# Two pre-activation layers on one core: the softmax without its maximum, checked after the fact instead of bounded beforehand

## The chip, the core and the metric

The kernel runs on one core of a Trainium2 chip. A core has a matrix engine (PE, with its weight loads shown as PEld), a vector engine (DVE), a scalar engine (ACT), GpSimd (POOL) and SyncE (SP), which in this kernel only issues transfers. Time is device time in microseconds (us). Each engine works through its own list of instructions in order; between engines, semaphores make one wait for another.

## The reference

The input x is 4 images of 16 channels of 256 x 256, in f32. Two layers, each of the form x + layer(GroupNorm(x)) with 8 groups of two channels:

```python
def _L0_conv_ref(x, conv_w, conv_b):          # conv_w: (16*25, 16, 3, 3)
    out = conv(x, conv_w, padding='SAME') + conv_b[None, :, None, None]
    logits = out.reshape(N, C, K * K, H, W)   # K = 5
    weights = jax.nn.softmax(logits, axis=2)
    return jnp.einsum('ncuij,ncuij->ncij', _unfold(x), weights)

x = x + _L0_conv_ref(_gn(x), L0_conv_conv_w, L0_conv_conv_b)
x = x + _L1_conv_ref(_gn(x), ...)   # silu and cubic B-splines of 3x3 patches, weighted sums, bias
```

`_unfold(x)` holds the 5 x 5 neighbourhood of each pixel. In layer 0 every pixel of every channel has 25 logits of its own, so the softmax is over 25 x 16 x 4 x 65,536 numbers. The second layer takes x1, the first layer's result.

## The kernel before, in words

**Prologue.** All four images are read for their group statistics. Image 0 comes in two halves of 2 MB that are kept (`held`), images 1 to 3 go through three buffers (`xin`); `load_x` (L498) issues them, five at the start and each further one when a half has been used. For each half DVE takes `bn_stats` (L635, L637); per image `group_stats` turns them into mean and rstd over two small matmuls with `ones` and a power on POOL (L165), from which the factors `nrm` and `nrz` follow (L655 to L658). At the same time the program finds a bound of the logits. ACT squares each half (`xq`, L644), 16 matmuls with an identity add the squares over the channels (`sq`, L647), DVE takes the maximum (`hm`, L650). The weights' squares (`aw`, `wps`) are summed once. From both, a chain of small operations (L660 to L690) computes whether every logit is small enough for an exponential without a maximum: `flag`.

Between these, `normalize` for the upper half of image 0 advances a piece at a time (`ahead`, two calls of `next` per group). It writes normalised x to DRAM in two layouts: by rows (`hs`, put from SP at L329) for the neighbourhoods, and transposed by columns (`hst`, and `hsl` with a high and a low part, L343) for the convolution. It uses two xp buffers and two buffers each of the transposed tiles.

**The branch.** Every engine loads `flag` (L1387) and branches (L1391). One arm runs both layers without a maximum, `layer0(False)`, the other runs both with it, `layer0(True)`, `layer1("g", ...)`. Only one arm runs.

**Layer 0.** 64 strips (4 images x 2 halves of 128 rows x 8 strips of 32 columns), rows on partitions, each strip in 8 steps of 4 columns. In each step PE makes the logits of 4 columns, two pairs with 2 matmuls a column (L974, L978), in three PSUM buffers; ACT takes the exponentials of each pair (L997); POOL multiplies them by the neighbourhood `u` (L1002); one step later (LAG) DVE adds numerators and denominators over the 25 (L813). `e`, which holds exponentials and products, has four buffers. After a strip follow, a few steps later each, `seed` (ACT: Ln and Exp of the denominators, L827, L829, an approximate reciprocal), `divide`, `refine`, `quotient` (DVE, L833 to L844), and per block of 128 columns `apply` (adds y to x in a transfer that POOL issues, L851), `store` (x1 to DRAM, L913) and `statistics` (ACT: sums of x1 and of its squares with accumulated output, L876). `step()` runs such delayed work when it is due, then `next(ahead)` advances `normalize` of the next image: densely, with a piece in every step, while image 0's strips run, more spread out for images 2 and 3. `x1` is stored from SP, but for the last strip.

SP issues, in the order of the program: columns `am` (four transfers) and `an` (one) for each half strip of 16 columns (L750, L758), `u` for each strip (L771), `xc` blocks (L791), xp loads (L321), and the puts of `normalize`. Two `an` buffers have rows of ones, set by DVE at the start of the layer (L736). `in_order` fixes the order of each engine's instructions within the two layers as written.

**Layer 1.** 64 units of 16 rows. Splines of x1 are built on DVE, ACT and POOL, and PE adds 3 x 3 convolutions (L1304, L1313). `scales(b, ...)` computes x1's group statistics for images 2 and 3 along the way, as pieces of the chain `more`. Outputs are stored by SP.

## Time and profile before

| what | us |
|---|---|
| three runs | 2863.25, 2865.0, 2867.84 (median 2865.0) |
| the profiled execution | 2861.58, of which span 2859.8; granted PE clock 0.982 |
| VectorE busy | 2774.1 (97%) |
| TensorE busy | 2716.4 (95%) |
| GpSimd busy | 2666.5 (93%) |
| ScalarE busy | 2124.1 (74%) |
| first transfer of columns `am` issued | 105.98 |
| first reduce of layer 0 starts | 125.61 |
| seed of the last strip | 1988.82 |
| last work on VectorE ends | 2853.5 |
| last store issued | 2854.77 |

The span runs from the first to the last instruction of the profiled execution; the device time beside it is that of the same execution. In a line of groups the columns are: line, engine, operation, output and inputs with their shapes, count, then busy time and the mean length of one (ns), then the idle time of the engine just before them and what ended most of it. A chain of waits is followed back from the last instruction, to what released each. A row of stretches gives busy times and, in brackets, numbers of instructions of each engine. Layer 0 starts at about 106 us and ends at about 1990, layer 1 follows it with some overlap on ACT and POOL.

### The profile page before, as it was taken

How to read it: one execution, taken by the hardware profiler on the slowest of the kernel's cores; microseconds unless marked ns; L12 is line 12 of the kernel's file. 1: busy time of each engine (PE TensorE's matmuls, PEld its weight loads, DVE VectorE, ACT ScalarE, POOL GpSimd, SP SyncE). 2: the span in 40 equal slices, each digit the busy share in tenths (PEclk: the TensorE clock that was granted, in tenths of full speed). 3: DMA queues.
4: the chain of work that ended last, by engine and by line, in shares of the span. 5: the costliest groups of instructions: out<-in, count | busy, mean ns of one | idle time of the engine just before them, and what ended most of it. 6: DMA issues, size and time to landing. Idle time of an engine off the chain costs nothing.

```text
span 2859.8 us, 39212 instructions
## 1 busy us (share of the span) xinstructions
PE 2716.4 (95%) x14282; PEld 1483.3 (52%) x14282; DVE 2774.1 (97%) x1821; ACT 2124.1 (74%) x2737; POOL 2666.5 (93%) x1096
## 2 busy tenths in 40 slices
PE   4699999999999999999999999996999999999999
PEld 3466666666666666666666666663343333323222
DVE  7699999999999999999999999999999999999996
ACT  6566777667767567676664655647999999999995
POOL 4399999999999999999999999999899999999995
PEclk8799999999999999999999999998999999999999
DMA  9877999979989779898886674866778787787783
GB/s 289 260 232 228 286 293 287 274 231 263 277 242 299 232 231 259 243 296 244 256 249 181 195 226 146 244 196 195 233 244 254 244 259 246 247 258 247 255 246 106
DMA packets 337663, 692.96 MB, mean 242 GB/s; under 512 B 29554, under 2 KB 254276, under 8 KB 287092
## 3 DMA queue, kind: packets, MB, share of 16 engines
q1 hardware_dynamic: 329796, 658.13, 74.5%
q0 software_dynamic: 7664, 32.23, 5.5%
q8 instruction: 115, 1.88, 0.3%
q14 instruction: 88, 0.72, 0.1%
HBM read 533.16 MB, written 121.15 MB: 229 GB/s over the span
## 4 chain that ended last, share of the span: by engine, by line
DVE 52%; PE 22%; issue 10%; ACT 6%; DMA 5%; POOL 2%; SPq 1%; DVEq 0%; POOLq 0%; ACTq 0%
DVE nd L813 42%; PE yp L1304 12%; PE lg L974 6%; PE yp L1313 3%; DVE ring L181 3%; DVE s L178 2%; PE lg L978 2%; DVE r L837 1%; DVE y L844 1%; DVE nd L833 1%; POOL e L1002 1%; DVE r1a L1148 1%; ACT xta L1139 1%; DMA xp<-in_x_dram 1%; ACT xtc L1139 1%
## 5 line engine op out<-in xcount | busy, mean ns | idle before, releaser
L1002 POOL TENSOR_TENSOR e<-e,u 128x1600 f32<-128x1600 f32 x512 | 1806.0, 3818 | 45.0 <-ACT e L997 27.8
L813 DVE TENSOR_REDUCE nd<-e 128x128 f32<-128x3200 f32 x512 | 1757.9, 3489 | 20.5 <-POOL e L1002 20.5
L974 PE MATMUL lg<-wm,am 128*128 128x400 f32 x4096 | 1731.6, 503 | 45.3 <-ACT e L997 33.3
L978 PE MATMUL lg<-wn,an 96*128 96x400 f32 x2048 | 1341.6, 655 | 0.8 <-DMA an<-hsl 0.8
L997 ACT ACTIVATE e<-lg 128x800 f32<-128x800 f32 x1024 | 810.3, 835 | 627.2 <-DVE nd L813 504.3
L974 PEld LDWEIGHTS lg<-wm,am 128*128 128x128 f32 x4096 | 750.7, 191 | 386.3 <-ACT e L997 113.1
L1304 PE MATMUL yp<-ring,wt 128*32 128x512 f32 x6144 | 721.2, 595 | 33.9 <-DVE ring L181 33.3
L978 PEld LDWEIGHTS lg<-wn,an 96*128 96x128 f32 x2048 | 386.0, 188 | 307.2 <-DMA an<-hsl 3.3
L1304 PEld LDWEIGHTS yp<-ring,wt 128*32 128x32 f32 x6144 | 227.9, 109 | 493.1 <-issue 429.3
L1161 POOL TENSOR_TENSOR s1b<-s1b,r1a 128x1024 f32<-128x1024 f32 (+1 forms) x96 | 192.6, 2038 | 0.0
L1161 POOL TENSOR_TENSOR s1a<-s1a,r1a 128x1024 f32<-128x1024 f32 (+1 forms) x96 | 192.3, 2037 | 0.0
L181 DVE SCALAR_TENSOR_TENSOR ring<-s,s1a 128x1024 f32<-128x1024 f32 x132 | 156.6, 1210 | 0.9
L181 DVE SCALAR_TENSOR_TENSOR ring<-s,s1b 128x1024 f32<-128x1024 f32 (+1 forms) x128 | 153.5, 1225 | 0.3
L876 ACT ACTIVATE z<-xc,nrm 128x256 f32<-128x256 f32 x240 | 144.3, 601 | 4.0
L1161 POOL TENSOR_TENSOR s1a<-s1a,r1b 128x512 f32<-128x512 f32 (+2 forms) x68 | 119.7, 1792 | 0.0
L1161 POOL TENSOR_TENSOR s1b<-s1b,r1b 128x512 f32<-128x512 f32 x64 | 114.8, 1820 | 0.0
L178 DVE SCALAR_TENSOR_TENSOR s<-xta,cb,s 128x1024 f32<-128x1024 f32 (+2 forms) x90 | 112.2, 1272 | 0.5 <-issue 0.4
L1157 POOL TENSOR_TENSOR s1a<-r1b 128x1536 f32<-128x1536 f32 (+1 forms) x31 | 86.7, 2795 | 26.2 <-ACT r1b L1146 26.2
L178 DVE SCALAR_TENSOR_TENSOR s<-xtb,cb,s 128x1024 f32<-128x1024 f32 (+2 forms) x85 | 107.2, 1287 | 1.9 <-ACT s L175 1.9
L178 DVE SCALAR_TENSOR_TENSOR s<-xtc,cb,s 128x1024 f32<-128x1024 f32 (+2 forms) x85 | 107.0, 1285 | 0.0
L175 ACT ACTIVATE s<-xta,cb 128x1024 f32<-128x1024 f32 (+2 forms) x90 | 96.4, 1085 | 12.5 <-DVE ring L181 11.0
L1157 POOL TENSOR_TENSOR s1b<-r1b 128x1536 f32<-128x1536 f32 (+1 forms) x32 | 86.4, 2699 | 17.5 <-ACT r1b L1146 17.5
(211 smaller groups left out, 2258.8 us busy)
## 6 DMA issues: line engine op xcount, KB each, us to landing
am<-hst SPq DMA_DIRECT2D x508, 259.8 KB
u<-hs SPq DMA_DIRECT2D x64, 1440.0 KB
an<-hsl SPq DMA_DIRECT2D x127, 519.5 KB
xta<-x1s SPq DMA_DIRECT2D x40, 1024.0 KB
xtb<-x1s SPq DMA_DIRECT2D x40, 1024.0 KB
xtc<-x1s SPq DMA_DIRECT2D x40, 1024.0 KB
x1s<-xc SPq DMA_DIRECT2D x30, 1024.0 KB
hs<-hsp SPq DMA_DIRECT2D x32, 576.0 KB
```

What stands on the lines that cost most here:

```text
L175: nc.scalar.activation(s, t, AF.Square, scale=-0.5, bias=cb)
L178: nc.vector.scalar_tensor_tensor(p, t, cb2, s, ALU.subtract, ALU.mult)
L181: nc.vector.scalar_tensor_tensor(f, p, 0.0, q, ALU.min, op)
L813: nc.vector.tensor_reduce(nd[:, :, :, j : j + JG].rearrange("p t c j -> p t j c"), e.rearrange("p t j m c d -> p t j c m d"), AX.XY, ALU.add,)
L876: nc.scalar.activation(z, v, f, scale=nrm[b][:, 0, g : g + 1], bias=nrm[b][:, 1, g : g + 1], accum_out=st1[b][:, t, g, columns_of(n) : col ...
L974: nc.tensor.matmul(lg[:, i, :NL], lhsT=am[:, o : o + P], rhs=wm.rearrange("p m c d -> p (m c d)"), start=True, stop=False,)
L978: nc.tensor.matmul(lg[:, i, :NL], lhsT=an[:, o : o + P], rhs=wn.rearrange("p m c d -> p (m c d)"), start=False, stop=True,)
L997: nc.scalar.activation(ev, lg[:, :, :NL], AF.Exp)
L1002: nc.gpsimd.tensor_tensor(e[:, 1].rearrange("p j m c d -> p j (m c) d"), e[:, 0].rearrange("p j m c d -> p j (m c) d"), uv, ALU.mult,)
L1157: nc.gpsimd.tensor_tensor(s1(n, a, z), r1(n, a, z), r1(n, a, z), ALU.mult)
L1161: nc.gpsimd.tensor_tensor(s1(n, a, z), s1(n, a, z), r1(n, a, z), ALU.mult)
L1304: nc.tensor.matmul(yp[t * M : (t + 1) * M], lhsT=wt[:, d, e].rearrange("p r o -> p (r o)"), rhs=ring[:, r0 + t * RT + d : r0 + t * RT + d ...
```

## The change

The bound and the branch ahead of the layers are taken out. Both layers run at once without a maximum; the sums are recorded and checked, and at the very end a branch repeats both layers with the maximum if the check fails.

- The prologue loads and measures images 0 and 1 alone, four loads of 2 MB. `xq`, `sq`, `hm`, `aw`, `wps`, `ms`, `bd` and all their work are gone.
- Images 2 and 3 are measured in layer 0, by a new generator `measure`, while images 1 and 2 have their strips: xp loads from SP, per group and half three ACT instructions (Identity with accumulated sum, a Copy of one element, Square with accumulated sum), then two small matmuls, DVE operations and a power on POOL. It pauses while `statistics` are due. `normalize` of the same image follows it in the chain, now dense for all images.
- `seed` gets a Copy over the denominators that accumulates their sum, a small bias in Ln, and an accumulated sum in Exp. The sums go to `seen`.
- `verdict`, in layer 1's chain `more` after `scales`, compares `seen` with 1e30 and computes `flag` (DVE, one matmul, DVE).
- `ubrow` moves from a lasting pool to the prologue's, `zero` becomes smaller with a broadcast source.

The stores of x1 are issued as before.

```diff
+    def factors(b, mean, rstd):
+        nc.vector.tensor_copy(nrm[b][:, 0], rstd)
+        nc.vector.scalar_tensor_tensor(nrm[b][:, 1], mean, -1.0, rstd, ALU.mult, ALU.mult)
+        nc.gpsimd.tensor_mul(nrz[b][:, 0], rstd, gsel_sb)
+        nc.vector.scalar_tensor_tensor(nrz[b][:, 1], rstd, EPS, rstd, ALU.mult, ALU.mult)
+
+    def measure(b, ptr, tiles, busy):
...
+        for h in range(NH):
+            load(0, h)
+        for _ in range(3):
+            yield
+        for q in range(C // QC):
+            for h in range(NH):
+                for k in range(QC // GC):
+                    while busy():
+                        yield
...
+                    nc.scalar.activation(v, v, AF.Identity, accum_out=s)
+                    nc.scalar.activation(m, s, AF.Copy, scale=-1.0 / n)
+                    nc.scalar.activation(v, v, AF.Square, bias=m, accum_out=s)
+                    yield
+                load(q + 1, h)
...
+        nc.tensor.matmul(
+            ps[0], lhsT=ones, rhs=moments[:, 0].rearrange("p g h -> p (g h)"),
+            start=True, stop=True,
+        )
+        yield
+        nc.vector.tensor_reduce(
+            mean, ps[0].rearrange("p (g h) -> p g h", h=NH), AX.X, ALU.add
+        )
+        nc.vector.tensor_scalar(mean, mean, -1.0 / NH, None, ALU.mult)
+        nc.vector.tensor_tensor(
+            d, moments[:, 0], mean.unsqueeze(2).to_broadcast([P, G, NH]), ALU.add
+        )
+        nc.vector.tensor_mul(d, d, d)
+        nc.vector.scalar_tensor_tensor(d, moments[:, 1], 1.0 / n, d, ALU.mult, ALU.add)
+        yield
+        nc.tensor.matmul(
+            ps[1], lhsT=ones, rhs=d.rearrange("p g h -> p (g h)"), start=True, stop=True
+        )
+        yield
+        nc.vector.tensor_reduce(
+            var, ps[1].rearrange("p (g h) -> p g h", h=NH), AX.X, ALU.add
+        )
+        nc.vector.tensor_scalar(var, var, 1.0 / NH, EPS, ALU.mult, ALU.add)
+        yield
+        nc.gpsimd.tensor_tensor(rstd, var, mhalf, ALU.pow)
+        yield
+        factors(b, mean, rstd)
+        yield
+
+    def verdict(psum):
+        low = seen.rearrange("p t n -> p (t n)")
+        least = stat1.tile([P, 1], F32, name="least")
+        nc.vector.tensor_scalar(low, low, 1e30, None, ALU.is_lt)
+        nc.vector.tensor_reduce(least, low, AX.X, ALU.min)
+        yield
+        ps = psum()[:, 0:1]
+        nc.tensor.matmul(ps, lhsT=ones, rhs=least, start=True, stop=True)
+        yield
+        bad = stat1.tile([1, 1], F32, name="bad")
+        nc.vector.tensor_scalar(bad, ps[0:1], 1.0 - 0.5 / P, None, ALU.is_lt)
+        nc.vector.tensor_copy(flag, bad)
+        yield
...
-        loaded = [load_x(n) for n in range(5)]
+        loaded = [load_x(n) for n in range(2 * NH)]
...
-        for b in range(B):
+        for b in range(2):
...
-                nc.scalar.activation(xq, t, AF.Square)
-                sq = pstat.tile([P, W], F32, name=f"sq_{n}", tag="sq")
-                for c in range(C):
-                    nc.tensor.matmul(
-                        sq, lhsT=idr, rhs=xq[:, c], start=c == 0, stop=c == C - 1
-                    )
-                nc.vector.tensor_reduce(hm[:, n : n + 1], sq, AX.X, ALU.max)
                 next(ahead, None)
-                if n >= NH and n + 3 < B * NH:
-                    loaded.append(load_x(n + 3))
...
             def seed(n, nd, xc):
                 r = prc.tile([P, C, SW], F32, name=f"r_{n}{arm}", tag="r")
-                nc.scalar.activation(r, nd[:, 0], AF.Ln)
+                nc.scalar.activation(
+                    nd[:, 0], nd[:, 0], AF.Copy, accum_out=seen[:, 1, n : n + 1]
+                )
+                nc.scalar.activation(r, nd[:, 0], AF.Ln, bias=tiny)
                 seeds[:1] = [newest(ACTE)]
-                nc.scalar.activation(r, r, AF.Exp, scale=-1.0)
+                nc.scalar.activation(
+                    r, r, AF.Exp, scale=-1.0, accum_out=seen[:, 0, n : n + 1]
+                )
...
-                    ahead = normalize(b + 1, ptr, tiles, dense=b == 0) if b + 1 < B else iter(())
+                    ahead = iter(())
+                    if b + 1 < B:
+                        ahead = normalize(b + 1, ptr, tiles, dense=True)
+                        if b > 0:
+                            ahead = chain(measure(b + 1, ptr, tiles, summing), ahead)
...
-    fast = nc.values_load(
+    layer1("", *layer0(False))
+    bad = nc.values_load(
         flag[0:1, 0:1], min_val=0, max_val=1,
         skip_runtime_bounds_check_because="a comparison's result",
     )
-    with tc.If(fast > 0) as small_logits:
-        layer1("", *layer0(False))
-    with small_logits.Else():
+    with tc.If(bad > 0):
         layer1("g", *layer0(True))
```

## The prediction, made before the changed kernel had run

> **What bounds the kernel now.** I read the engine table, the chain of waits, the groups, the busy time by stretches, then the waits of VectorE (DVE) and the timeline at the places that the change touches.
>
> ```profile
> DVE 52%; PE 22%; issue 10%; ACT 6%; DMA 5%; POOL 2%; SPq 1%; DVEq 0%; POOLq 0%; ACTq 0%
> ...
> L1002 POOL TENSOR_TENSOR e<-e,u 128x1600 f32<-128x1600 f32 x512 | 1806.0, 3818 | 45.0 <-ACT e L997 27.8
> L813 DVE TENSOR_REDUCE nd<-e 128x128 f32<-128x3200 f32 x512 | 1757.9, 3489 | 20.5 <-POOL e L1002 20.5
> ...
> L997 ACT ACTIVATE e<-lg 128x800 f32<-128x800 f32 x1024 | 810.3, 835 | 627.2 <-DVE nd L813 504.3
> ```
>
> ```profile
> 0.00:50.00 50.00, 17.95 (x78) 15.76 (x78) 32.94 (x131) 26.93 (x33) 31.80 (x85) 0.93 0.96 281
> 50.00:100.00 50.00, 29.00 (x138) 25.27 (x138) 38.17 (x125) 41.78 (x64) 3.79 (x5) 0.66 0.93 294
> ...
> 286.00:572.00 286.00, 276.53 (x990) 180.74 (x988) 280.90 (x109) 212.77 (x378) 276.88 (x88) 0.99 0.98 285
> 572.00:858.00 286.00, 282.52 (x1003) 181.33 (x1002) 286.00 (x110) 200.79 (x334) 285.02 (x88) 1.00 0.85 253
> ```
>
> Columns of the second view: stretch, length, busy time (instructions) of PE, PE loads, DVE, ACT, POOL, granted clock, DMA share, GB/s. In layer 0 DVE decides: from 572 on it is busy 286.00 of 286. ACT waits 504 us for DVE, so added ACT work is free as long as no single delay uses up the pipeline's lead. Layer 0 has 512 steps; 28.94 us a strip of eight gives 3.617 a step. At 916.1 a reduce frees an e buffer; exps end 1.6 us later, the POOL product takes 3.5, the reduce 3.4 and hand-overs about 0.5: 9.0 of the 14.5 us that four buffers last, so the **lead is about 5.5 us**. Before 125.61 there is no reduce: the prologue is a serial 126 us, to which this chain belongs:
>
> ```profile
> 99.93 1.65 POOL rstd_x L165
> ...
> 104.72 0.15 DVE flag L690
> 104.89 0.50 POOLq L1387
> ...
> 106.64 0.58 SPq L750
> ...
> 117.47 10.68 DMA xp<-in_x_dram
> ```
>
> Image 3's statistics end at 101.6, bound and flag take until 104.87, the branch about 1.1, and only then are layer 0's columns (am) loaded; the first matmul is at 111.04, the first product at 122.06 (after u, issued at 112.46).
>
> **The change, part by part.**
>
> *Prologue.* Gone are five squares of 3.62 on ACT in 36 to 100 (18.1 us) with aw (1.06), DVE's statistics of images 2 and 3 (four halves of 8 x 0.61, about 19), the squares' matmuls, four of six 2 MB loads (8.4 MB at 290 GB/s, 29 us of DMA in a stretch with a share of 0.93), and the tail 99.93 to 105.98. What stays sets the new end: ACT is busy 55.66 us in 36 to 100, without squares and aw 36.5. Image 0's factors, at 35.76 now, come about 2 us sooner. So ACT ends no sooner than 34 + 36.5 = 70.5; its waits for DVE there (2.77, 1.43, 1.02, 2.20, 0.69) add 8.1: 78.6. The last put and its landing take some 6 more (98.33 to 105.98 now holds 1.4 us of ACT and put, the rest is covered): am at about 86 instead of 105.98, **-20**. Bounds: if DVE's waits go too, -28; if the pace of tile buffers and puts (two buffers, each put waited for) holds and only tail and one square in two go, -11. The two an memsets (1.79 each) move to where DVE is free; moved ubrow memsets and ident are not on the path.
>
> *Layer 0, DVE.* Measuring images 2 and 3 puts ten small DVE operations per image between reduces. Their like in the prologue (L155 to L163, L655 to L658) take 0.15 to 0.19 and start 0.2 apart: 1.75 an image, **+3.5** (2.4 to 4), all on the path.
>
> *Layer 0, ACT.* A measured step holds two exps (1.57 together at 287.32) and Identity and Square over 512 elements (0.58 each as L827), two accumulator reads, bounded by this row's 0.19,
>
> ```profile
> L876 ACT ACTIVATION_READ_ACCUMULATOR z<-xc,nrm 128x1 f32 x240 | 46.4, 193 | 0.0
> ```
>
> and a one-element Copy (0.20 as L382): 1.75, with gaps up to 2.15. 3.3 to 3.7 against 3.617: ACT has no spare time over 16 steps an image, and every eighth step a seed takes 2.2 instead of 1.2 (a Copy over 512 and two reads more). Each xp buffer is reloaded after its second step and read again two steps later. Cycle: 14.47 us of four steps, less one step (3.62) and 1.8 of work, leaves 9.0 for the load; the two loads that the chain of waits holds took 10.68 (at 117.47, share 0.81) and 17.97 (at 277.49, share 0.98). I take 10.68, since the stretch had 0.85: three reloads late by 1.7 are 5.0, within the lead of 5.5. **+1** for both images (0 to 43: three times 9.0 less 5.5, twice). The seed's extra 1.0 in the other strips is hidden by ACT's waiting.
>
> *Layer 0, SyncE.* The reload of an image's lower half waits in SP for ACT's fourth measured step, and the next block's four am and one an are queued behind it. PE frees their buffer just before that step's exps, so they go out up to 1.57 + 2.15 = 3.7 later than now. They last until the next block, 14.5 us on; from first issue to first matmul they took 5.1 (105.98 to 111.04). The sum, 8.8, is covered: 0; were loads as slow as 10.7, 14.4 would still just be covered. The stores of x1 stand in the same queue as before: 0.
>
> *Layer 0, PE and POOL.* The second ones-matmul stands two steps after the first, behind DVE's deviations: PE gives up its lead and sits idle some 7 us. What follows is seen at 288.89, where ACT waited 6.65 us for xp:
>
> ```profile
> 297.18 1.70 PE L974 MATMUL lg<-wm,am 128*128 128x400 f32 x2 [4.40 <-ACT e L997]
> ```
>
> This and the next pair took 1.70 and 1.47 instead of 0.84. After the deviations DVE holds two reduces (7.0); the next product needs two slow pairs of columns (3.3), an exp (0.85), the product (3.5) and 0.3: 7.95. About 1 late. POOL's power (1.65) then eats POOL's regained lead, 0.3 more. **+2.6** for two images (0 to 6).
>
> *Layer 0, dense normalisation of images 2 and 3.* Image 1 is dense now: DVE waits 5.1 us for POOL in 286 to 572, at a DMA share of 0.98. Images 2 and 3, spread out, show none. Part of the 5.1 is that one late xp load. **+4** for two (0 to 10.2).
>
> *Layer 1 and end.* The last strip's divide already waits 1.28 for ACT (1990.04); the seed's extra Copy lies in it: **+1.0** (0 to 1.3). The verdict's four DVE operations and its matmul stand in units where DVE and PE are both full: **+0.7** (0 to 1.2). The flag's load and branch now stand behind all: now from the flag's end (104.87) to the first instructions behind (105.51 to 106.24) it took 0.65 to 1.4; partly under the last store's flight (2854.77 to 2859.8): **+0.5** (0 to 1.4).
>
> The Trainium skill, "Advanced Engine Details and Errata", "Control Flow Timing", gives a compare-and-branch as about 108 ns. The rows above are six to thirteen times that, since load and synchronisation are in them; by the page the last term would be 0.1 and the sum 0.4 lower.
>
> **Sum**: -20 + 3.5 + 1 + 2.6 + 4 + 1.0 + 0.7 + 0.5 = -6.7. The profiled execution took 2861.6 (span 2859.8, the rest around it) and would take 2854.9; it lies 3.4 under the median of 2865.0, against which runs are compared: 2858.3, rounded **2858**.
>
> **Rivals.**
> *The prologue gives only half* (-10): puts and SyncE's queue, not ACT, set its end. For it: two tile buffers, ACT waiting for DVE in five places; weight loads ws wait in SP among large loads (up to 4.06 us each). Against: those waits fall with the loads. -10 + 13.3 = +3.3: 2868.
> *ScalarE uses up the lead* while it measures. Place: the 16 steps of images 2 and 3, at the xp reload; it decides once a reload takes over 9.0 + 5.5/3 = 10.9 us. For it: 10.68 is just below, 17.97 well above. Against: mean share 0.85. At 14.3, midway, 3 x 5.3 - 5.5 = 10.4 an image: +21 instead of +1, so **2878, slower**.
> *The change doesn't do what it says*: the sums fail their test and both layers are run again. Then the time is over 5,500. For these inputs, normalised logits of a few units, exponentials are far from 1e30; nothing in the trace shows them.
>
> **How the numbers follow.** About 0.2% (5.7 us) is what a measurement here can tell from no change: faster is below 2859.3, slower above 2870.7. Forecast 0.50 (of it 0.40 faster, 0.10 within), half a prologue 0.25 (0.03, 0.15, 0.07), ScalarE 0.24 (0, 0.03, 0.21), repetition 0.01. Faster 0.43, within 0.28, slower 0.29. The forecast's own range is 2846 to 2868 (prologue -28 with the sum's other terms low but not all at zero, and -14 with them near the values taken plus 3). The whole range reaches to the second rival: 2846 to 2879.
>
> **What would show it.** First am issue near 86 and first reduce near 105 (now 125.61): prologue. DVE's waits for POOL's products in the strips of images 1 and 2, about 570 to 1490, in which 2 and 3 are measured and normalised: about 3 an image by the forecast (2.6 + 4 over two), over 10 by the second rival, with ACT waiting for xp behind it. PE idle at the second ones-matmul: 5 to 8 us each, DVE's wait near 1. The wait before the last divide: 2.3 instead of 1.28. The forecast is wrong if the first reduce comes after 115, or if layer 0 from first reduce to last grows by more than 20.

## The result and the profile after

The changed kernel is slower: 2887.7 us (median of 2882.99, 2884.55, 2890.79 and 2891.38) against 2864.1 (2860.67 to 2867.84), a ratio of 1.0081 with a 95% interval of 1.0059 to 1.0104. That is 9 us above the upper end of the predicted range. The profiled execution of after is the quickest of the four: 2882.99, span 2881.0, granted clock 0.979. Its span is 21.2 longer than that of before, and 21.2 is what has to be explained.

The chain of waits by engines, and the three costliest groups of after (busy time, mean ns of one, idle time in front and what ended most of it):

```profile
DVE 47%; PE 23%; issue 10%; ACT 7%; DMA 7%; POOL 5%; SPq 1%; DVEq 0%; ACTq 0%; POOLq 0%
...
L1051 POOL TENSOR_TENSOR e<-e,u 128x1600 f32<-128x1600 f32 x512 | 1804.6, 3799 | 77.8 <-ACT e L1046 63.3
L850 DVE TENSOR_REDUCE nd<-e 128x128 f32<-128x3200 f32 x512 | 1757.1, 3476 | 46.8 <-POOL e L1051 46.5
L1046 ACT ACTIVATE e<-lg 128x800 f32<-128x800 f32 x1024 | 823.6, 835 | 548.0 <-DVE nd L850 277.9
```

The big operations themselves cost what they did: 512 reduces 1757.1 (1757.9 before), 512 products 1804.6 (1806.0). The idle times are what differ. DVE now waits 46.5 for products instead of 20.5 in the whole run, POOL 63.3 for exps instead of 27.8, and ACT has 79 us less of its slack (548.0 of 627.2). So the work between the large operations and the hand-over from engine to engine have to be looked at.

The stretches of the prologue and of layer 0 in after (length, busy time of PE, PE loads, DVE, ACT and POOL with instruction counts, granted clock, DMA share, GB/s):

```profile
0.00:50.00 50.00, 7.35 (x28) 5.84 (x28) 32.02 (x120) 17.40 (x32) 31.77 (x85) 1.00 0.87 255
50.00:100.00 50.00, 23.58 (x81) 16.66 (x82) 15.17 (x44) 25.72 (x58) 3.42 (x19) 0.66 0.82 254
...
286.00:572.00 286.00, 279.77 (x998) 182.70 (x996) 275.44 (x105) 218.87 (x400) 276.70 (x88) 0.99 0.94 277
572.00:858.00 286.00, 269.57 (x950) 174.44 (x949) 285.82 (x117) 223.56 (x423) 274.14 (x85) 0.98 0.82 245
```

In the second 50 us DVE's work fell from 38.17 to 15.17 and ACT's from 41.78 to 25.72: the prologue is shorter, am leaves at 82.97 instead of 105.98 and the first reduce starts at 102.60 instead of 125.61, 23.0 earlier. But see 572 to 858: DVE is just as full as before (285.82 of 286.00), while POOL fell from 285.02 to 274.14 and PE from 282.52 to 269.57. A bounding engine that is fully busy while the others do less is spending its time on something that isn't the main work. This is the whole of layer 0, from the first reduce to the start of the last divide, first of before and then of after:

```profile
125.61:1990.04 1864.43, 1808.52 (x6336) 1154.81 (x6334) 1857.98 (x733) 1229.06 (x2051) 1831.61 (x566) 0.99 0.82 242
```

```profile
102.60:2010.08 1907.48, 1812.12 (x6344) 1167.42 (x6342) 1875.86 (x753) 1340.41 (x2403) 1837.64 (x572) 0.98 0.81 242
```

Layer 0 grew by 43.05. DVE got 20 more instructions and 17.9 us more of busy time, 0.9 us each, where the prediction had 0.175. Three groups of it (two instructions each, one per measured image) are not like their rows in the prologue:

```profile
L246 DVE SCALAR_TENSOR_TENSOR nrz<-rstd 128x8 f32<-128x8 f32 x2 | 7.1, 3561 | 0.0
L307 DVE TENSOR_SCALAR var<-var 128x8 f32<-128x8 f32 x2 | 4.9, 2455 | 0.1
L243 DVE COPY nrm<-rstd 128x8 f32<-128x8 f32 x2 | 2.4, 1212 | 0.0
...
L246 DVE SCALAR_TENSOR_TENSOR nrz<-rstd_x 128x8 f32<-128x8 f32 x2 | 0.3, 152 | 0.0
```

The last line is the same source line with the same shape for images 0 and 1 in the prologue: 152 ns there, 3561 ns in layer 0. The other part of the growth is in waits:

```profile
DVE nd L850 <- POOL e L1051: 46.5, 16, 23.2
DVE nd L875 <- ACT r L869: 7.6, 1, 7.6
```

The longest one, 23.2, is the start of layer 0 and lies ahead of the first reduce. The 23.3 that are left stand against 5.1 before. The wait for the last divide is 7.57 instead of 1.28.

| part of the span | forecast | measured |
|---|---|---|
| start to first reduce | -20 | -23.0 |
| DVE's small operations in layer 0 | +3.5 | +17.9 |
| DVE's waits for products (lead 2.6, dense 4, ACT 1) | +7.6 | +18.2 |
| wait before the last divide | +1.0 | +6.3 |
| from the last divide on (verdict, end branch) | +1.2 | +1.2 |
| remainder |  | +0.6 |
| sum | -6.7 | +21.2 |

### The profile page after: what moved, and what is told of

It reads as the page before. It is cut to its first block, busy times and chain, and to the rows that moved or that the text cites. A ratio compares the mean times of both kernels' runs of the same rounds, so it can differ in the third digit from the quotient of the medians.

```text
span 2881.0 us, 39240 instructions
## 1 busy us (share of the span) xinstructions
PE 2691.3 (93%) x14150; PEld 1486.9 (52%) x14150; DVE 2763.2 (96%) x1735; ACT 2204.9 (77%) x3077; POOL 2665.2 (93%) x1096
## 4 chain that ended last, share of the span: by engine, by line
DVE 47%; PE 23%; issue 10%; ACT 7%; DMA 7%; POOL 5%; SPq 1%; DVEq 0%; ACTq 0%; POOLq 0%
DVE nd L850 36%; PE yp L1353 10%; PE lg L1023 8%; POOL e L1051 3%; DVE ring L182 3%; DVE s L179 3%; PE yp L1362 2%; PE lg L1027 2%; ACT xtc L1188 1%; DVE r1a L1197 1%; ACT xtb L1188 1%; DMA an<-hsl 1%; DVE nd L875 1%; DVE r L879 1%; DVE y L886 1%
## 5 line engine op out<-in xcount | busy, mean ns | idle before, releaser
L1051 POOL TENSOR_TENSOR e<-e,u 128x1600 f32<-128x1600 f32 x512 | 1804.6, 3799 | 77.8 <-ACT e L1046 63.3
L850 DVE TENSOR_REDUCE nd<-e 128x128 f32<-128x3200 f32 x512 | 1757.1, 3476 | 46.8 <-POOL e L1051 46.5
L1046 ACT ACTIVATE e<-lg 128x800 f32<-128x800 f32 x1024 | 823.6, 835 | 548.0 <-DVE nd L850 277.9
L1023 PEld LDWEIGHTS lg<-wm,am 128*128 128x128 f32 x4096 | 760.8, 192 | 388.7 <-ACT e L1046 89.4
L1027 PEld LDWEIGHTS lg<-wn,an 96*128 96x128 f32 x2048 | 388.1, 190 | 317.2 <-DMA an<-hsl 12.1
L1353 PEld LDWEIGHTS yp<-ring,wt 128*32 128x32 f32 x6144 | 239.3, 108 | 483.9 <-issue 414.0
L1206 POOL TENSOR_TENSOR s1a<-r1b 128x1536 f32<-128x1536 f32 (+1 forms) x31 | 86.6, 2794 | 24.5 <-ACT r1b L1195 24.5
```

Of the source, the lines that this page charges most:

```text
L850: nc.vector.tensor_reduce(nd[:, :, :, j : j + JG].rearrange("p t c j -> p t j c"), e.rearrange("p t j m c d -> p t j c m d"), AX.XY, ALU.add,)
L1023: nc.tensor.matmul(lg[:, i, :NL], lhsT=am[:, o : o + P], rhs=wm.rearrange("p m c d -> p (m c d)"), start=True, stop=False,)
L1027: nc.tensor.matmul(lg[:, i, :NL], lhsT=an[:, o : o + P], rhs=wn.rearrange("p m c d -> p (m c d)"), start=False, stop=True,)
L1046: nc.scalar.activation(ev, lg[:, :, :NL], AF.Exp)
L1051: nc.gpsimd.tensor_tensor(e[:, 1].rearrange("p j m c d -> p j (m c) d"), e[:, 0].rearrange("p j m c d -> p j (m c) d"), uv, ALU.mult,)
L1206: nc.gpsimd.tensor_tensor(s1(n, a, z), r1(n, a, z), r1(n, a, z), ALU.mult)
```

## The experiments

Each run is compared with runs of the kernel before on the same chip, whose medians there lay between 2863.1 and 2863.5. Line numbers in the profiles are those of the kernel at hand. Edits are against after where nothing else is said.

### One suspect each

**e1: one operand in PSUM.** Mean and raw variance stay in PSUM, POOL writes the reciprocal straight into its factor, the last factor is a Square on ACT.

```diff
-        d = stat1.tile([P, G, NH], F32, name=f"dev_{b}", tag="dev")
-        mean, var, rstd = small(G, "mean"), small(G, "var"), small(G, "rstd")
+        var = stat1.tile([P, G], F32, name=f"var_{b}", tag="varm")
+        rstd = nrm[b][:, 0]
+        mean = bank[:, 2, 0:G]
+        raw = bank[:, 2, G : 2 * G]
...
-        factors(b, mean, rstd)
+        nc.vector.scalar_tensor_tensor(nrm[b][:, 1], mean, -1.0, rstd, ALU.mult, ALU.mult)
+        nc.gpsimd.tensor_mul(nrz[b][:, 0], rstd, gsel_sb)
+        nc.scalar.activation(nrz[b][:, 1], rstd, AF.Square, scale=float(EPS) ** 0.5)
```

> The factors of images 2 and 3 computed so that no small DVE operation beside a running GpSimd product reads two SBUF operands or copies SBUF to SBUF (mean in PSUM, rstd written by GpSimd straight into nrm, nrz's second half by ScalarE); nothing else differs from the changed kernel. Theory 'shared port': the changed kernel's L246 (3.56 us each), L243 (1.2) and L307 (2.1 to 2.8) are long only because GpSimd's product holds something that they need. Then each of their replacements takes 0.15 to 0.25 us. L307's time should turn into a wait for GpSimd's product (its e was not ready sooner), so the gain is that of L243 and L246: 2 x 4.4 = 9 us, up to 14 if L307's goes too; 2874 to 2879 against 2887.7 (0.9963 to 0.998 of before's 0.2% steps above 1: ratio to before 1.003 to 1.005). Rival 'slow instruction': these operations are slow in themselves or wait for their input; then the replacements are as long, and the time stays at 2888 (ratio 1.008).

Measured: 2885.6, ratio 1.0085 (1.0072 to 1.0098), no gain. Yet the operations did what was expected: 0.15 to 0.18 us each, and DVE's busy time in layer 0 fell by 12.4 to 1863.46. The waits took it over:

```profile
DVE nd L853 <- POOL e L1054: 60.3, 26, 22.6
```

Without the start of the layer 37.7, where after had 23.3: the 14.4 are more than what the instructions gave up. While DVE stood in its small operations POOL went ahead; without that stay it meets POOL's gap itself. One of two delays at the same place, taken away alone, gives nothing.

**e2: the seed's Copy behind the mark.** `in_order` reads `seeds`, which marks where ACT goes over to layer 1's work. After marks Ln; the accumulating Copy that stands ahead of it waits for the last reduce.

```diff
-                nc.scalar.activation(r, nd[:, 0], AF.Ln, bias=tiny)
                 seeds[:1] = [newest(ACTE)]
+                nc.scalar.activation(r, nd[:, 0], AF.Ln, bias=tiny)
```

> The last strip's Copy stands behind the layer-1 work of ScalarE instead of in front of it (the mark that ties the seed to that work is taken from the Copy, not from Ln); one line differs. Theory 'wrong place': the last divide waits 7.57 us instead of 1.28 because the Copy waits 5.5 us for the last reduce and 5.6 us of layer-1 activations stand between it and Ln. Then the wait before the last divide falls to 2.0 to 2.8 us, and the time by about 5: ratio to before about 1.006. Rival 'seed too long': the wait is that of a longer seed; then it stays above 6 us and the time at 1.008.

ACT at the end of layer 0 in after shows what the edit is about (start, length, last the idle time ahead and who ended it):

```profile
2002.55 0.63 ACT L864 ACTIVATE nd<-nd 128x512 f32<-128x512 f32 x1 [5.50 <-DVE nd L850]
...
2003.18 1.77 ACT L1195 ACTIVATE r1b<-xta,cb 128x1792 f32<-128x1792 f32 x1
2004.98 1.70 ACT L1203 ACTIVATE s1a<-r1b 128x1792 f32<-128x1792 f32 x1
2006.58 2.14 ACT L176 ACTIVATE s<-xta,cb 128x1024 f32<-128x1024 f32 x2
2008.66 0.67 ACT L867 ACTIVATE r<-nd,tiny 128x512 f32<-128x512 f32 x1
```

The Copy (L864) waits 5.50 with layer 1's activations queued behind it, and these 5.6 us then run ahead of Ln, for which the last divide waits. In e2 the divide's wait is 2.25, as expected. The time is not shown to be better: 2890.7, ratio 1.008 (1.006 to 1.010), over a wide span of runs (2878 to 2897). In the profiled one the same six small operations took 26.9 instead of 14.4 (L246 10.8, L243 9.6, L307 6.5), and the verdict's comparison 6.9 instead of 0.6. How long such an operation lasts is not a constant.

**e3: images 2 and 3 normalised in a spread order.**

```diff
-                        ahead = normalize(b + 1, ptr, tiles, dense=True)
+                        ahead = normalize(b + 1, ptr, tiles, dense=b == 0)
```

> Images 2 and 3 are normalised spread out, as before the change, after being measured as in the changed kernel; one expression differs. Theory 'dense': DVE's waits for GpSimd's products in the strips that normalise images 2 and 3 (6.49, 0.69, 4.59 and 0.62 us) come from transfers issued close together, with columns late behind them; then these go, -12 us: ratio to before about 1.004. Rival 'measuring': they come from the lead that measuring has used up; then 8 us or more of waits stay between 600 and 1500.

2914.2, ratio 1.0169 (1.0151 to 1.0186), the slowest of all variants of after, which neither theory had. After the measuring steps a spread normalisation no longer fits into its image, and the rest is drained in one go ahead of the next image's strips. DVE in the run's timeline:

```profile
1032.63 13.94 DVE L850 TENSOR_REDUCE nd<-e 128x128 f32<-128x3200 f32 x4 [6.76 <-POOL e L1051]
1053.08 3.49 DVE L850 TENSOR_REDUCE nd<-e 128x128 f32<-128x3200 f32 x1 [6.51 <-POOL e L1051]
```

Two more such waits, 6.55 and 8.72, stand at 1523 and 1546. So dense is needed once images are measured here, and this run can't price it.

**e4: no sums.** The seed's Copy and both accumulations are left out, `seen` is filled with 1.0.

```diff
-                nc.scalar.activation(
-                    nd[:, 0], nd[:, 0], AF.Copy, accum_out=seen[:, 1, n : n + 1]
-                )
```

> The seed's Copy and both accumulated sums are left out, so the sums aren't recorded (the record holds ones); the rest is the changed kernel. Theory 'seed': the extra 1.0 us of ScalarE per strip costs 6 us of waits in the strips of image 0, where the normalisation of image 1 is dense (11.0 in the changed kernel against 5.1 before), and 6.3 at the last divide; both go: -12, ratio to before about 1.004, divide's wait near 1.3. Rival 'earlier start': image 1's extra waits come from the layer starting 23 us sooner among other transfers; then they stay near 11 and only the 6 at the last divide go: ratio about 1.006.

2883.8, ratio 1.0058 (1.0036 to 1.0081). The last divide waits 1.38 and DVE's waits in image 0's strips fall from 11.0 to 7.6, but its waits in 600 to 1500 grow from 12.4 to 21.0, the longest of them 8.47 at 926. By the waits the longer seed costs some 3.4 on image 0 and 6 at the end; most of this gain is lost again further on.

### Room, transfers, and the place of images 2 and 3

**e5: more steps between the parts of the measurement** (two ahead of the first ones-matmul, four ahead of the second, three ahead of the power).

```diff
+        for _ in range(4):
+            yield
         nc.tensor.matmul(
             ps[1], lhsT=ones, rhs=d.rearrange("p g h -> p (g h)"), start=True, stop=True
         )
```

> In measure, the first ones-matmul comes two steps later, the second four steps after the deviations and the power three steps after the variance; the rest is the changed kernel. Theory 'lead given up': PE's wait for the deviations (7.8 and 6.9 us in the changed kernel) and with it GpSimd's idle time of 9.0 and 7.5 go, since PE, ScalarE and GpSimd keep their lead over DVE. GpSimd is busy nearly as long as DVE (1838 of 1907 us), so what it loses there comes back only as DVE's waits in the following dense stretch: with it 8 to 15 us of the 12 us of waits between 700 and 1500 and of the 14 us of long small operations go; ratio to before 1.003 to 1.0055. Rival 'late columns': the waits near 926 and 1405 come from SyncE alone; then they stay, and the ratio stays at 1.007 to 1.009.

PE's wait for the deviations (14.7 in two) is gone, as it should be, and the time is worse: 2899.6, ratio 1.0124 (1.011 to 1.0139). POOL is now in an unbroken run of products when DVE's small operations come, and three lines are held up for 24 us (L295, L311 and L243: 13.5, 6.0 and 4.5). The largest is the scaling of the mean, which took 0.17 in after, where POOL happened to be idle (it waits 8.98 and 7.47 around the two places):

```profile
L295 DVE TENSOR_SCALAR mean<-mean 128x8 f32<-128x8 f32 x2 | 13.5, 6728 | 0.1
```

**e6: the zeros of images 2 and 3 early**, from POOL's queue in the prologue, where SyncE had issued them in layer 0.

```diff
-        moves = moves if held is None and part is None else []
+        moves = moves if b == 1 and held is None and part is None else []
```

> The twelve zero fills of the borders of images 2 and 3 are issued by GpSimd in the prologue, as image 0's are, instead of by SyncE among the dense puts; the rest is the changed kernel. Theory 'late columns': SyncE stands 8.17 us at the fill at 894.42 with am and an behind it, PE then waits 3.2 for am, and DVE 6.49. Without the fills among the puts PE's waits for am and an in 600 to 1500 fall from 12 us to under 5, and DVE's waits near 926 and 1405 to under 2 each: -8, ratio 1.004 to 1.0065. Rival 'queue full whatever stands there': SyncE is held by the puts before it; another transfer then stands for 8 us in its place, PE still waits 8 us or more, ratio 1.007 to 1.009.

2887.2, ratio 1.0083 (1.007 to 1.0096), as the rival had it. PE's waits in 600 to 1500 still name the columns:

```profile
PE mps L300 <- DVE dev L298: 14.6, 2, 7.8
...
PE lg L1024 <- DMA am<-hst: 10.0, 6, 4.4
PE lg L1028 <- DMA an<-hsl: 2.8, 9, 1.1
```

In after these are 9.0 and 3.2 (0.6 together before), so the zeros are not what makes columns late. The first reduce comes later in e6, at 107.3; layer 0 takes 1906.3, against 1907.5 in after.

**e7: e1, e2, e5 and e6 together.**

> Measuring spaced out as in e5, operands in PSUM as in e1, the Copy behind the mark as in e2, fills early as in e6. If the stalls add up as named (lead given up and late columns 12 to 16 of waits, small operations 10, mark 5), layer 0 shrinks from 1907 to about 1880, and with a prologue of 23 less than before the time is about 2860: ratio 0.996 to 1.001. If each only uncovers the next, as e1's did, it stays above 1.004.

2887.7, ratio 1.008 (1.0062 to 1.0097): nothing gained. One operation with two SBUF operands had been left, the square of the deviations, and with POOL never idle it now pays:

```profile
L300 DVE TENSOR_TENSOR dev<-dev 128x16 f32<-128x16 f32 x2 | 12.4, 6184 | 0.1
```

**e8: all four images in the prologue**, as in before but still without bound, flag and branch there.

```diff
-        for b in range(2):
+        for b in range(B):
...
-                            ahead = chain(measure(b + 1, ptr, tiles, summing), ahead)
```

> Images 2 and 3 are loaded and measured in the prologue as before, and normalised spread out as before; the bound stays out, the sums, the check and the branch at the end stay in. Theory 'measuring in layer 0 is what costs': layer 0 from first reduce to last divide takes about 1876 (1864 before, 6 at the last divide, 6 for the seed in image 0's strips), the first am is issued at 85 to 98, and the time is 2855 to 2866: ratio 0.997 to 1.001. Rival 'the seed and the new order cost': layer 0 stays above 1895, ratio above 1.004.

2878.2, ratio 1.0048 (1.0035 to 1.0061), about 10 better than after. The first reduce comes at 123.2: without the bound the prologue is only 2.4 shorter. Images 2 and 3 are normalised in a spread order again, as in before. Layer 0 takes 1881.8, still 17.4 more than before: waits in image 0's strips 15.1, for the last divide 7.6.

### The operation by itself, and the end

**e9: e8 without sums. e10: e8 with the denominators' sum taken by Ln itself**, so that no Copy is needed, and the upper half of image 0 normalised to its end before images 2 and 3 are measured.

```diff
-                nc.scalar.activation(r, nd[:, 0], AF.Ln, bias=tiny)
+                nc.scalar.activation(
+                    r, nd[:, 0], AF.Ln, bias=tiny, accum_out=seen[:, 1, n : n + 1]
+                )
```

> As e8 (all images measured in the prologue, normalised as before) and the sums left out too: the record holds ones, the seed is Ln and Exp as before; what stays of the change is that the bound is out and the check and the branch stand at the end. Theory 'the sums cost e8 its 17 us': image 1's waits (15.1 in e8) fall to 4 to 8, the last divide's (7.6) to 1.3, layer 0 to 1862 to 1870, and with the first reduce 2 us earlier than before the time is that of before: ratio 0.997 to 1.001. Rival 'order or check at the end': it stays at 1.003 or more.

> As e8, but the sum is accumulated by Ln itself instead of by a Copy (so a sum that overflows is still found as infinite, while the threshold of 1e30 for the sums themselves is gone), and image 0's upper half is normalised to its end before images 2 and 3 are measured. Theory: the seed is 0.4 us longer than before instead of 1.3, its first instruction is the marked one again, so the last divide waits 1.4 to 1.8 and image 1's waits are 5 to 9; am is issued at 85 to 95 and the first reduce starts at 103 to 115, since the measuring of images 2 and 3 lies beside the first loads of layer 0: ratio 0.993 to 0.998, faster than both kernels. Rival 'the loads of x set the start': first reduce at 120 or later, ratio 0.999 to 1.002.

e9: 2872.5, ratio 1.0031 (1.002 to 1.0042); e10: 2873.2, 1.0029 (1.0017 to 1.0042). In e9 layer 0 is back at 1865.7 (1864.4 before); what is left stands behind it: 879 from the last divide on, where before had 869.8. The verdict's comparison over 128x128 takes 6 us more than in after's profile (0.612 there):

```profile
L318 DVE TENSOR_SCALAR seen<-seen 128x128 f32<-128x128 f32 x1 | 6.9, 6928 | 0.0
```

Over the profiles of after, e1 to e10 it took 0.61 (after, e5, e6), 4.18 (e1) or 6.9 (the other seven).

**m1 and m2: the operation alone.** To the kernel before, one 128x8 multiplication per strip of layer 0 is added, 64 in all, with a result that nothing reads. In m1 both operands are in SBUF; in m2 one of them is in PSUM.

```diff
+                nc.vector.scalar_tensor_tensor(
+                    extra, nrm[0][:, 0], 1.0, nrm[0][:, 1], ALU.mult, ALU.mult
+                )
```

```diff
-                    extra, nrm[0][:, 0], 1.0, nrm[0][:, 1], ALU.mult, ALU.mult
+                    extra, r[:, 0, 0:G], 1.0, nrm[0][:, 1], ALU.mult, ALU.mult
```

> The kernel before, with one more small DVE operation (128x8, product of two SBUF operands into SBUF) ahead of each strip's quotient, 64 in all; its result is not used. Theory 'shared port': while a GpSimd product runs, it waits until that ends, and POOL is busy 98% of layer 0; a random place in a product of 3.5 us would make 1.75 each, and as GpSimd starts its next product at once it may be passed over: 64 x 1 to 3.5 = 64 to 224 us. Rival 'small operation': 0.16 each, 10 us: ratio 1.0035.

> As m1, with one operand in PSUM (a corner of r) instead of SBUF. Theory 'shared port': 0.15 to 0.2 each, 64 x 0.16 = 10 us: ratio 1.003 to 1.004. Rival 'any small operation between the reduces waits': as long as m1's.

Their groups, m1 and then m2:

```profile
L845 DVE SCALAR_TENSOR_TENSOR extra<-nrm 128x8 f32<-128x8 f32 x64 | 241.2, 3769 | 0.0
```

```profile
L845 DVE SCALAR_TENSOR_TENSOR extra<-r,nrm 128x8 f32<-128x8 f32 x64 | 10.0, 156 | 0.0
```

Same engine, same size, same place. m1 takes 3092.5, which is 229.3 more than before or 3.58 an operation (ratio 1.0797, 1.077 to 1.0824); m2 takes 2866.2, 3.1 more (ratio 1.0010, 1.0001 to 1.0020). The price is not in what the instruction computes but in where its operands lie.

**f1: the verdict's comparison on POOL.**

```diff
-        nc.vector.tensor_scalar(low, low, 1e30, None, ALU.is_lt)
+        nc.gpsimd.tensor_scalar(low, low, 1e30, None, ALU.is_lt)
+        yield
```

> The changed kernel with the verdict's comparison (128x128, SBUF to SBUF) on GpSimd instead of DVE, half a step of layer 1 earlier; nothing else differs. Theory 'shared port': in the changed kernel's profile this comparison met a free port (0.61 us), in four other profiles it took 4.2 to 6.9 us, which is also why its runs fall into 2883 to 2885 and 2890 to 2892. Then layer 1 takes 869 to 872 us from the last divide on in every run, the runs' spread shrinks and the median falls by 3 to 5: ratio 1.0055 to 1.007. Rival 'spread from layer 0's waits': median and spread stay, 1.008.

2885.7, ratio 1.0075 (1.0061 to 1.0089). It takes 0.54 there, the part from the last divide on 870.1, and the runs lie within 4.9 us instead of 8.4. A gain in time isn't shown by it: its interval and that of after overlap.

### What remains when all of it is mended

**f2: e1, e5 and f1 together, the deviations' square with one factor in PSUM, and the sum in Ln. f7: the same without e5's added steps.**

```diff
-        nc.vector.tensor_mul(d, d, d)
+        dp = bank[:, 3, 0 : G * NH].rearrange("p (g h) -> p g h", h=NH)
...
+        nc.vector.tensor_mul(dp, dv, dp)
```

> Images 2 and 3 measured in layer 0 with no DVE operation that has two SBUF operands or copies SBUF to SBUF (also the square of the deviations, now with one operand in PSUM), the tail spaced as in e5, the sum accumulated by Ln, the comparison on GpSimd. Theory: what is left over e8 with the same seed is then the dense stretches of images 2 and 3 (12 to 17 us of DVE's waits) and nothing of the tail; PE waits nowhere for the deviations, every small operation takes under 0.3 us; first reduce at 100 to 107, layer 0 takes 1880 to 1888, time 2855 to 2866: ratio 0.997 to 1.001. Rival 'ScalarE measures too much': GpSimd still waits 30 us or more for exponentials in 600 to 1500, layer 0 stays above 1895, ratio 1.003 or more.

> f2 without the spaced tail: the second ones-matmul again two steps behind the first, the power one step behind the variance. It prices the lead that PE and GpSimd give up there, by itself. Theory of the prediction: PE waits 7 us for the deviations, DVE loses about 1 us for each image at once; with GpSimd's later waits counted (its 16 us of idle time have to come from somewhere) 3 to 10 for both: ratio 1.001 to 1.0035 against f2's 0.9998. Rival 'free': GpSimd makes it up in the spread of the strips, ratio below 1.0005.

f2: 2863.6, ratio 0.9998 (0.9989 to 1.0007), 24 us better than after and equal to before. Its small operations are back at the prologue's rows, though POOL is in a run of products at every one of them:

```profile
L302 DVE TENSOR_TENSOR mps<-dev,mps 128x16 f32<-128x16 f32 x2 | 0.4, 179 | 0.1
L314 DVE TENSOR_SCALAR var<-mps 128x8 f32<-128x8 f32 x2 | 0.3, 166 | 0.1
```

By the profiles f2's layer 0 takes 1887.0, 20.5 less than that of after: DVE's busy time is 13.7 lower and the last divide waits 6.0 less, while the waits for products ahead of it are as long as in after (22.7 and 23.3 without the start).

f7 is 2876.1, ratio 1.0039 (1.0026 to 1.0053): 12.4 us above f2 by the medians, and this is the price of the lead where nothing else holds DVE up there. It shows in DVE's waits, f2 and then f7, of which 23.6 and 24.5 are the start of the layer:

```profile
DVE nd L862 <- POOL e L1062: 46.3, 19, 23.6
```

```profile
DVE nd L856 <- POOL e L1056: 63.7, 23, 24.5
```

POOL while image 2 is measured, at the product behind the second ones-matmul, in f7 and then in f2:

```profile
686.87 7.00 POOL L1056 TENSOR_TENSOR e<-e,u 128x1600 f32<-128x1600 f32 x2 [6.84 <-ACT e L1051]
```

```profile
686.71 3.53 POOL L1062 TENSOR_TENSOR e<-e,u 128x1600 f32<-128x1600 f32 x1 [0.96 <-ACT e L1057]
```

The bracket is POOL's idle time. In f7 PE has stood behind the deviations (waits of 11.2 in two) and POOL lost 6.84, and 6.86 at image 3. Right behind these places DVE waits 6.5 in all; its other waits, the longest 6.65 at 1408, stand elsewhere, and that POOL's lost time makes them longer isn't shown.

**f4: e10 with f1 and a fourth load buffer in the prologue. f6: f2 with image 2 measured in the prologue**, so that only image 3 is left to layer 0 (with the loads and the order of f4 in the prologue).

```diff
-        name="xin", bufs=3
+        name="xin", bufs=4
```

> As e10 (all images measured in the prologue, image 0 normalised first, sum by Ln), with four buffers for x instead of three, so that no load of x is queued behind image 0's puts, and the comparison on GpSimd. Theory: e10's last load of x stood behind the puts (DVE waited 12.1 us for it and the first reduce came at 125.8); with it gone the first reduce is at 108 to 118; layer 1 takes 870 as in the kernel before; layer 0 1866 to 1870: time 2849 to 2862, ratio 0.995 to 0.9995. Rival 'x sets the start': the loads take the same time wherever they stand in the queue and the first reduce stays at 120 or later: ratio 0.999 to 1.001.

> As f2 (no small DVE operation in GpSimd's way, tail spaced, sum by Ln, comparison on GpSimd), with only image 3 measured in layer 0: image 2 is loaded (four buffers) and measured in the prologue and normalised spread out as before; image 0 is normalised to its end before image 2 is measured. Theory: layer 0 loses only one dense stretch, 8 to 10 us of DVE's waits instead of 19; the prologue's gain is 16 to 21 of 24 (first reduce at 104 to 110): time 2852 to 2860, ratio 0.996 to 0.9985. Rival 'two more loads set the start': first reduce at 115 or later, ratio 0.999 to 1.002.

f4: 2862.2, ratio 1.0 (0.9991 to 1.0009); f6: 2866.0, 1.0007 (0.9997 to 1.0016). In f4 the first reduce comes at 120.5, layer 0 takes 1865.7 and the rest 871.8; in f6 the first reduce comes at 112.1. The three ways of sharing out the images (f2: two in layer 0, f6: one, f4: none) end within 4 us of each other and of before: what an image saves ahead of layer 0 it costs within it. No version beats before.

## Why the prediction was wrong

It took the side that the prologue spoke for. The prologue's term was nearly right; layer 0 took 43 where the terms placed in it held 12.1.

*Prologue, -20: right in size, wrong in reason.* It gave 23.0, well within the step's bounds of 11 to 28 (the working's own terms, 78.6 and 6, add up to 84.6 rather than 86; am left at 82.97). The working let ACT, freed of five squares, set the new end. e8 has no squares either, keeps the loads and statistics of images 2 and 3, and gains only 2.4 of the 23.0. So with all images kept, taking out the bound with its squares, flag and branch is hardly worth anything, and putting off two images brings the other 20.6; what that would bring with the bound kept wasn't tried. That the size came out has some luck in it. The half-prologue rival is out.

*DVE's small operations, +3.5: the step that failed.* It took their price, 0.15 to 0.19, from rows in the prologue, with bounds of 2.4 to 4, and 17.9 came. There POOL has no products to compute; in layer 0 it is busy for 98% of the time. DVE and POOL side by side in after, DVE first:

```profile
690.58 2.78 DVE L307 TENSOR_SCALAR var<-var 128x8 f32<-128x8 f32 x1
...
700.77 1.22 DVE L243 COPY nrm<-rstd 128x8 f32<-128x8 f32 x1
701.91 0.24 DVE L244 SCALAR_TENSOR_TENSOR nrm<-mean,rstd 128x8 f32<-128x8 f32 x1
702.07 3.56 DVE L246 SCALAR_TENSOR_TENSOR nrz<-rstd 128x8 f32<-128x8 f32 x1
```

```profile
689.82 7.01 POOL L1051 TENSOR_TENSOR e<-e,u 128x1600 f32<-128x1600 f32 x2 [8.98 <-ACT e L1046]
...
698.43 3.53 POOL L1051 TENSOR_TENSOR e<-e,u 128x1600 f32<-128x1600 f32 x1
...
702.09 13.95 POOL L1051 TENSOR_TENSOR e<-e,u 128x1600 f32<-128x1600 f32 x4
```

Add start and length. DVE's variance ends at 693.36, as the first of POOL's two products does (half of 7.01 after 689.82 is 693.33). The Copy ends at 701.99, POOL's product at 701.96. The short one after it, 0.24, falls where POOL has no product. The last one ends at 705.63, the first of POOL's four (a quarter of 13.95 after 702.09) at 705.58. Each held-up operation ends when a product ends: it waits for POOL, and the profile shows it as busy, so no view of waits names it. m1 and m2 show that the place of the operands decides. They do so for an operation with one input, too: the variance's scaling took 2.46 on the mean from SBUF to SBUF in after (L307) and 0.17 from PSUM to SBUF in f2 (L314), beside POOL's products both times. Six operations of this kind took 14.4; the other fourteen took 0.17 to 0.24 each, 2.6 together, as forecast for such operations.

The Trainium skill, "SBUF — State Buffer", section "SBUF: two separate sides", states this: a pair of ports shared by VectorE and GpSimd is held by whichever starts first for its whole instruction, and the VectorE operations that need it are those with two SBUF inputs and those in a mode that uses two ports. The prediction didn't weigh it. m1 agrees, with 3.58 us in the time for each operation beside a product of 3.5; that an operation can wait for more than one product, as the longest of m1 with 8.57 did, isn't in it. Which of the one-input operations run in such a mode no run shows. By that rule up to eight operations an image are exposed (five with two inputs in SBUF, three that take one from SBUF to SBUF); at half a product of wait each that would have been 28 for two images, an estimate, and a reason to forecast slower.

*The lead, +2.6: mis-sized.* The mechanism was seen where it was forecast: PE waits 7.8 and 6.9 for the deviations (forecast some 7), POOL then stands idle for 9.0 and 7.5. Its price is 12.4 (f7 against f2), twice the upper bound of 6. The step let POOL regain its lead. But in layer 0 of before POOL is busy 1831.6 us against DVE's 1858.0: it has 26 us of slack over 512 steps, 0.05 a step, and 7 us are not regained within an image of 128 steps. (This reason is worked out, not tried.) The two failed terms also hid each other: e1 mends only the operands and e5 only the lead, and neither helps, since a DVE that doesn't stop meets POOL's gap and a POOL that doesn't pause blocks DVE. In after both delays fall into the same stretch, so the lead's price is not a further part of the 21.2: none of DVE's longer waits there stands at the deviations (682 and 1161), they stand at 928 (6.49) and 1405 (4.59). f2, which mends both, is 24 us better, of which 6.0 in its profile are the last divide's.

*Dense normalisation, +4, and ScalarE, +1.* DVE waits 12.4 in 600 to 1500, where these terms and the lead had 7.6 together. In f2, with the lead kept, 16.1 are there, so late columns are the likely cause: PE waits 18.0 for am and an in f2 and 12.2 in after, 0.6 before. The prediction costed SyncE's queue at nothing ("The sum, 8.8, is covered: 0"), and that step was wrong too. It isn't the zeros (e6) and a spread order is worse (e3); the reloads of xp and x1's stores in the same queue remain, together with the longer queue that a dense order makes; which of them it is wasn't tried. The seed's extra time outside the last strip was put at nothing as well ("is hidden by ACT's waiting"). In image 0's strips DVE waits 11.0, before 5.1; without the sums it is 7.6 (e4), and from e8 to e9, which differ in the sums alone, it falls from 15.1 to 6.0. For the measuring steps ACT was right: a measured step takes 3.14 of the 3.62, its waits for xp are 5.4 in all, and the ScalarE rival, though its 2878 came nearest, is not what happened.

*The last divide, +1.0: mis-sized.* It cost 6.3. The extra Copy was counted for its 0.6; that it stands ahead of the mark which ends layer 0's order on ACT, so that 5.6 us of layer 1's work get in ahead of Ln, was not seen. e2 (wait 2.25) and the sum in Ln (1.6 in e10 and f2) show it.

*Verdict, +0.7, and end branch, +0.5.* Together 1.2 in the profiled execution, as forecast, but by luck for the verdict: its comparison reads and writes SBUF and takes 0.6 or up to 6.9, as it meets a product or not. From the issue of the last store to the end of the program it is 7.1 instead of 5.6, so the branch cost 1.5 rather than 0.5, and nothing of the verdict's 0.7 shows. The Trainium skill's 0.1 for a compare-and-branch ("Advanced Engine Details and Errata", "Control Flow Timing"), which the prediction had set beside its own term, was further off than that.

*Repetition* didn't take place; the time excludes it.

## What to carry to other kernels

Price an added instruction by a row from the stage where it will run, with the neighbours that are busy there: the same 128x8 operation was 0.15 us beside an idle GpSimd and 3.56 beside a busy one, and a PSUM operand made it 0.16 again. Where two engines are nearly equally full, a gap in the second can be nearly as dear as one in the first (here two of 7 us cost 12), so give a serial chain between engines enough steps that nobody stands behind it. And when two delays lie at one place, taking either away may show nothing; try them together before clearing either.

## What the runs showed of the hardware

A small VectorE operation may be passed over by GpSimd more than once. In m1 the mean is 3.77 us and the longest 8.57, though one product takes 3.5. DVE and then POOL of m1 around one of them:

```profile
590.83 3.48 DVE L814 TENSOR_REDUCE nd<-e 128x128 f32<-128x3200 f32 x1
594.23 6.59 DVE L845 SCALAR_TENSOR_TENSOR extra<-nrm 128x8 f32<-128x8 f32 x1
600.74 0.67 DVE L848 TENSOR_TENSOR y<-nd,r 128x512 f32<-128x512 f32 x1
```

```profile
586.25 14.53 POOL L1006 TENSOR_TENSOR e<-e,u 128x1600 f32<-128x1600 f32 x4
606.54 3.53 POOL L1006 TENSOR_TENSOR e<-e,u 128x1600 f32<-128x1600 f32 x1 [5.76 <-ACT e L1001]
```

DVE asks at 594.23, in the third of POOL's four back-to-back products (3.63 each, so it runs from 593.51 to 597.15), and gets through only when the fourth ends, at 600.78: the next product went in ahead of it, and DVE's turn came when POOL had none left. The two scalings of the mean in e5 (5.30 and 8.15) also end only where POOL's unbroken runs of 12 and 14 products do, at 690.37 and 1180.84; in after the held-up operations got in between two products. With a full POOL the price is therefore anything from nothing (147 ns is the shortest of the 64) to more than two products. The multiplication right behind it, L848, takes its usual 0.67: it has r in PSUM, as all three operations of the quotient have, and those are not held up in any strip (0.67 to 0.69 each in after between 600 and 1550). The large operations of layer 0 aren't held up by POOL's products, the added ones were.

An operation on a single column wasn't held up in the kernel before: one of 128x1 took 0.15 at 1697.75 while POOL was in a product. No run here took this further.
